# Spectral mixing: batches brought innermost on chip, block-diagonal operand filled by transfers, mirrored columns computed by symmetry

## The chip, the cores and the metric

The kernel runs on one core of one Trainium2 chip, as one program and one launch. The metric is device time in microseconds (us). A core has five engines that each work through their own instructions in order and wait for one another by semaphores: TensorE (PE in the profile; its weight loads are listed as PEld), VectorE (DVE), ScalarE (ACT), GpSimd (POOL) and SyncE (SP), which here only issues transfers. POOL issues transfers too. All transfers of a core run on 16 shared DMA engines. SBUF is the on-chip memory with 128 partitions, called lanes here; PSUM is the memory that TensorE writes its products to.

## The reference

Input `x` has 16 batches, 16 channels and 256 x 256 points. Two residual layers follow each other; the change lies in the first, a pole-residue (Laplace) operator on the group-normalised input:

```python
alpha = jnp.fft.fft2(x, axes=(-2, -1))
A  = 1.0 / (omega1[:, None, None, None] - weights_pole1[None])
Bm = 1.0 / (omega2[:, None, None, None] - weights_pole2[None])
S  = jnp.einsum('ikpq,oikp,xikq->oxik', weights_residue, A, Bm)
output_residue1 = jnp.einsum('biox,oxik->bkox', alpha, S)      # the mix
...
x1 = jnp.fft.ifft2(output_residue1, s=(Ny, Nx), axes=(-2, -1)).real
```

For every frequency (o, x) a 16 x 16 complex matrix `S` mixes the channels i into channels k, for all 16 batches b. As `x` is real, only row frequencies 0 to 128 are computed. The second residual layer (convolutions, mish, an involution and a gate) is not touched.

## The kernel before

`forward` runs four stages one after the other. They hand their data over through tensors in DRAM.

**layer0_forward** (0 to about 1377 us of the profile) computes the spectrum. For every batch b and group of four channels, `rows` transforms the image's rows: products `pu` (L207) with the table `fy`, a copy `right` of one half on ACT (L222), and two additions on DVE (L224) that write the sum and the difference of the two image halves, transposed, into the tile `u`. `columns` (L302 ff.) transforms the other axis from `u` (products `px`, L313), scales on ACT into `o` (L320), and POOL writes `o` to the DRAM tensor `al` (L329). `al` is laid out as group of four row frequencies, real/imaginary part, 64 lanes (row frequency, channel), batch, column frequency.

**layer0_mix** (about 1377 to 2785 us) does the mix in 33 groups g of four row frequencies each. PE, ACT, DVE and POOL follow the order written out by hand at the end of the function (`tc.manual_schedule`). One group consists of:

- `poles(av)`: three DVE products (L640) that spread the pole table into a block-diagonal operand `lt`.
- `residues(lt, s, k0)`, eight times: 16 products of 64 x 32 weights (L656) each, which give the matrices `S` of two output channels; copied to `s` by DVE (L665) or ACT (L667) in turn.
- `spread` and `expand`: the spectrum is loaded from `al` in four quarters of the batches (`alc`, four transfers of 128 KB each, L607, issued by SP), and 16 masked copies (10 on DVE, L619; 6 on ACT, L617) put it into `alb`, the block-diagonal operand: each lane holds one row frequency's channel, and of the four column blocks only its own is not zero. The mask `m4` multiplies the others by zero. `alb` has one buffer.
- `mix(s, y, between)`: 256 products with 128 x 32 weights from `s` and 64 columns from `alb` (L679), in four chunks, each copied to `y` by ACT (L686).
- `turn(y, f)`, four times: eight transposes (L695), copied to `yt` by DVE (L701) and ACT (L699).
- `columns(g, f, yt)`, four times: the inverse transform along the columns. 16 products of 64 x 128 weights with 256 columns of the table `ix` (L714), alternating between lanes 0-63 and 64-127; even and odd points come separately. ACT copies the odd part (L723), DVE writes the sum and the difference (L726, L727) into `o` (tile name `h`, five buffers), and POOL issues four transfers to the DRAM tensor `hd` (L734). For f = 3 the products are interleaved with the next group's `mix` (`between`), behind its second and third chunk.

The stretch from a group's `mix` to the end of its fourth chunk is called the mix section below, and the rest, up to the next `mix`, the f section. In a profile every product of 32-bit numbers appears as two weight loads and two products.

**layer0_back** (2785 to 3422 us) finishes the inverse transform, and **layer1** (3422 us to the end) is the second residual layer.

## Time and profile before

| what | value |
|---|---|
| median of 3 runs | 6919.82 us (6911.33 to 6925.25) |
| the profiled execution's own time | 6939.37 us |
| span of its profile | 6937.6 us |
| mean granted TensorE clock | 0.967 |
| busy in the span: PE, DVE, ACT, POOL | 92%, 79%, 53%, 52% |
| layer0_mix, one group (2003.88 to 2045.67 us) | 41.79 us |
| of it mix section / f section | 16.09 / 25.70 us |
| busy in this group: PE, DVE, ACT, POOL | 36.93, 26.55, 24.32, 13.70 us |

Times of stages are read from tables of busy time by window. A line of a group of instructions gives kernel line, engine, operation, output and inputs, shapes, count, then the time during which at least one of them ran and the mean duration of one, then the idle time of the engine just before them and what ended it. As instructions overlap at their ends, the busy time divided by the count is what one costs in a row, and the mean is what it takes by itself.

### The profile page before, as it was taken

Reading aid. Unit: us, or ns where it says so; the run is one execution under the profiler, and the core shown is the slowest. Engines: PE = TensorE matmul, PEld = TensorE weight load, DVE = VectorE, ACT = ScalarE, POOL = GpSimd, SP = SyncE. Lnnn points to the kernel's source line nnn. Section 1 sums busy time; section 2 is a strip of 40 time slices with the busy share of each in tenths; the row PEclk is TensorE's granted clock in tenths of the full one; section 3 lists DMA queues with packets and bytes.
Section 4 is the critical chain, followed back from the end, with each engine's and each line's share of the span. In section 5 each row is a group of like instructions: output and inputs, shape, how many; then the busy total and the mean of one; then the engine's idle time right before and its main releaser. Section 6 shows DMA issues by size and latency. Waiting matters only on the chain.

```text
span 6937.6 us, 153382 instructions
## 1 busy us (share of the span) xinstructions
PE 6375.2 (92%) x59944; PEld 3583.2 (52%) x59944; DVE 5451.1 (79%) x10057; ACT 3703.9 (53%) x5732; POOL 3635.8 (52%) x4614
## 2 busy tenths in 40 slices
PE   7899989978888888899789999999999999999996
PEld 5777777766766677677533333333333333333331
DVE  8888987356666666788788888888888888888885
ACT  1223333355655555222376666666666666666671
POOL 2334544523333333666665666666766566665563
PEclk9999999989999999999899999999999999999998
DMA  3444434433333333999877898888988889988886
GB/s 95 124 123 122 122 112 119 113 123 104 111 108 111 110 104 93 318 327 326 281 209 231 272 285 261 264 274 277 286 267 261 272 267 285 287 262 262 272 272 211
DMA packets 715941, 1443.97 MB, mean 208 GB/s; under 512 B 101338, under 2 KB 523542, under 8 KB 672950
## 3 DMA queue, kind: packets, MB, share of 16 engines
q1 hardware_dynamic: 567030, 959.77, 45.0%
q0 software_dynamic: 148192, 474.40, 21.8%
q8 instruction: 478, 7.83, 0.5%
q14 instruction: 241, 1.97, 0.1%
HBM read 877.12 MB, written 556.47 MB: 207 GB/s over the span
## 4 chain that ended last, share of the span: by engine, by line
PE 65%; DVE 20%; DMA 5%; issue 5%; ACT 4%; POOL 1%; SPq 0%; DVEq 0%; ACTq 0%; POOLq 0%
PE c2ps L1201 17%; PE c L1053 14%; PE pd L1121 13%; PE pg L679 4%; PE ph L714 3%; DVE alb L619 3%; ACT wide L1101 3%; PE px L313 2%; PE pu L207 2%; PE py L876 2%; PE pr L1080 2%; PE pv L214 2%; DVE u L224 2%; PE py L877 2%; DVE st L174 1%
## 5 line engine op out<-in xcount | busy, mean ns | idle before, releaser
L1101 ACT ACTIVATE wide<-c,b 32x512 f32<-32x512 f32 x2176 | 1479.6, 680 | 311.6 <-PE c L1053 263.5
L1132 DVE TENSOR_TENSOR top<-pd,t 32x512 f32<-32x512 f32 x2176 | 1504.0, 691 | 52.6
L1053 PE MATMUL c<-z,w 102*128 102x512 f32 x2048 | 999.7, 620 | 110.7 <-ACT wide L1101 89.3
L1113 POOL COPY wide<-wide 32x1031 f32<-32x1031 f32 (+1 forms) x576 | 579.7, 1006 | 881.5 <-ACT wide L1101 854.4
L1129 DVE TENSOR_TENSOR t<-pd,r 64x512 f32<-64x512 f32 x1088 | 744.1, 684 | 345.3 <-PE pd L1121 298.2
L1121 PE MATMUL pd<-wide,dw 128*128 128x512 f32 x2048 | 988.6, 604 | 12.0 <-DVE top L1132 11.0
L734 POOL DMA_DIRECT2D hd<-h x512 | 434.8, 856 | 955.0 <-DVE h L727 937.0
L1053 PEld LDWEIGHTS c<-z,w 102*128 102x128 f32 x2048 | 371.7, 192 | 697.5 <-issue 462.5
L1201 PE MATMUL c2ps<-rows,c 128*32 128x512 f32 x6144 | 721.6, 602 | 5.6 <-DVE odd L1228 5.6
L1121 PEld LDWEIGHTS pd<-wide,dw 128*128 128x128 f32 x2048 | 380.9, 192 | 572.2 <-issue 418.5
L1114 POOL COPY wide<-wide 32x1031 f32<-32x1031 f32 (+1 forms) x576 | 576.0, 1000 | 33.5
L1072 ACT ACTIVATE bot<-c,b 128x512 f32<-128x512 f32 x544 | 344.4, 684 | 462.6 <-issue 381.4
L714 PE MATMUL ph<-ix,yt 64*128 64x256 f32 x4128 | 507.9, 394 | 17.6 <-DVE yt L701 14.7
L313 PE MATMUL px<-wxn,u 128*64 128x256 f32 x4224 | 481.5, 379 | 2.4 <-ACT o L320 2.4
L207 PE MATMUL pu<-fy,eo 128*128 128x128 f32 x2048 | 436.2, 297 | 42.0 <-DVE u L224 35.2
L714 PEld LDWEIGHTS ph<-ix,yt 64*128 64x128 f32 x4128 | 419.6, 192 | 89.9 <-ACT s L667 29.6
L679 PE MATMUL pg<-alb,s 128*32 128x64 f32 x16896 | 311.6, 237 | 154.1 <-issue 71.8
L1201 PEld LDWEIGHTS c2ps<-rows,c 128*32 128x32 f32 x6144 | 174.8, 108 | 513.5 <-issue 404.5
L889 POOL TENSOR_TENSOR x<-x,o 128x512 f32<-128x512 f32 x256 | 324.4, 1267 | 217.3 <-DVE o L888 197.5
L619 DVE TENSOR_SCALAR alb<-alc,m 128x1024 f32<-128x1024 f32 x330 | 424.1, 1415 | 0.0
L214 PE MATMUL pv<-at,eo 128*128 128x128 f32 x2048 | 423.0, 291 | 0.0
L726 DVE TENSOR_TENSOR h<-ph,odd 128x256 f32<-128x256 f32 x258 | 113.4, 440 | 389.4 <-ACT odd L723 389.4
(221 smaller groups left out, 11460.2 us busy)
## 6 DMA issues: line engine op xcount, KB each, us to landing
rows<-cf SPq DMA_DIRECT2D x128, 2176.0 KB
z<-zn SPq DMA_DIRECT2D x768, 257.8 KB
cf<-top POOLq DMA_DIRECT2D x512, 240.0 KB, 6.9
cf<-bot POOLq DMA_DIRECT2D x96, 840.0 KB, 10.8
alc<-al SPq DMA_DIRECT2D x528, 128.0 KB
zn<-zb SPq DMA_DIRECT2D x128, 516.0 KB
o<-zn SPq DMA_DIRECT2D x128, 516.0 KB
z<-in_x SPq DMA_DIRECT2D x64, 1024.0 KB
```

The source lines that it names most:

```text
L313: nc.tensor.matmul(ps[64 * k : 64 * k + 64, :, h], lhsT=u[:, h, part, g0 + j + k].rearrange("p f c -> p (f c)"), rhs=wxn[:, h, part], star ...
L619: eng.tensor_scalar(dst, t, m4[:, j : j + 1], None, ALU.mult)
L679: nc.tensor.matmul(ps[32 * q : 32 * q + 32, x], lhsT=s[:, i].rearrange("p v k -> p (v k)"), rhs=alb[:, i].rearrange("p j b -> p (j b)"), s ...
L714: nc.tensor.matmul(ph[q][:, e], lhsT=yt[lanes, i].rearrange("p t k -> p (t k)"), rhs=ix[lanes, i], start=n == 0, stop=n == 3,)
L1053: nc.tensor.matmul(ps[:, a], lhsT=w, rhs=z[:k, c : c + 2, 0:N], start=True, stop=True)
L1101: nc.scalar.activation(self.feat[64 - 32 * q : 96 - 32 * q, f, self.groups[g], :H], ps[q][32 * f : 32 * f + 32], AF.Mish, bias=b1[0][32 * ...
L1113: nc.gpsimd.tensor_copy(flat[0:32, f, 1:m], flat[64:96, f, 0 : m - 1])
L1114: nc.gpsimd.tensor_copy(flat[96:128, f, 0 : m - 1], flat[32:64, f, 1:m])
L1121: nc.tensor.matmul(ps, lhsT=dwt if self.tail else dw, rhs=self.feat[:, f, cs, :H], start=True, stop=True,)
L1129: nc.vector.tensor_tensor(t[64:128], ps[:64], self.r[:, cs], ALU.mult)
L1132: nc.vector.tensor_tensor(self.top[32 * f : 32 * f + 32, cs, q], ps[lanes], t[lanes], ALU.add)
L1201: nc.tensor.matmul(ps[32 * j : 32 * j + 32], lhsT=w[:, blk], rhs=src[:, 4 * j + blk : 4 * j + blk + 4, x : x + H], start=(i, blk) == (0, 0 ...
```

## The change

The mix works on other data layouts, and its hand-written order changes with them.

- **Order of lanes.** In `layer0_forward` the tile `u` keeps the channel ahead of the row frequency, and a lane of the spectrum is now (row frequency, channel) with the frequency slowest in a table order that puts even numbers first. The DVE additions (L224) therefore write runs of four numbers instead of single numbers 64 bytes apart; their reads step through `pu` and `right` by 32 numbers instead of by 128. `al` is laid out anew: runs of 2 KB are written where there were runs of 1 KB, and runs of 1 KB are read where there were runs of 4 KB.
- **Batches innermost, then transfers.** Instead of 16 masked copies, four plain copies (`interleave`: two on DVE, two on ACT) bring the batches innermost into a new tile `alx` (one buffer), from quarters `alc` (two buffers, one transfer of 512 KB each). `place` issues four SBUF-to-SBUF transfers from SP, of 512 KB each, which write only the blocks of `alb` that are not zero: lanes f, f + 4, f + 8, ... go to block f. The zeros are written once, by two memsets ahead of the stage. A group's `place` stands behind the `mix` of the group before.
- **Mirrored columns.** With a transform at half-integer points, the column x and its mirror image differ only by the sign of one part, so `columns` multiplies by 128 columns of `ix` instead of 256. The symmetric and the antisymmetric parts then give all points: DVE writes the sum and (backwards) the difference into a new tile `w`, and one more addition on DVE and one subtraction on POOL make `o` (now four buffers).
- **Order.** `turn(y, f + 1)` is done ahead of `columns(g, f)`; `residues` stand two ahead of each turn, the last one behind the last turn; the copies of `interleave` for group g + 2 stand behind the `columns` of f = 1 and f = 2.

```diff
-                        pu[:, xh, e].rearrange("p v m -> p (v m)"),
+                        pu[:, xh, :, e],
...
-                    u[:, h, :, :64, :, ch],
-                    pu[:, 0].rearrange("p e v m -> p v m e"),
-                    right.rearrange("p e v m -> p v m e"),
+                    u[:, h, :, : NF - 1, ch],
+                    pu[:, 0].rearrange("p v e (m g) -> p v g (e m)", m=2),
+                    right.rearrange("p v e (m g) -> p v g (e m)", m=2),
...
-                    out=al[g0 + k : g0 + n : 2, v, :, b].rearrange("g p x -> p g x"),
-                    in_=o[64 * k : 64 * k + 64, :w, v],
+                    out=al[g0 // 2 + k, :, v, :, b, :w].rearrange("h c g x -> h c (g x)"),
+                    in_=o[64 * k : 64 * k + 64, v, :w].rearrange("p g x -> p (g x)"),
...
-    alb = cp.tile([P, N, 4, nb], F32, name="alb")
+    alb = cp.tile([P, 4, N, nb], F32, name="alb")
+    nc.vector.memset(alb[:, :2], 0.0)
+    nc.gpsimd.memset(alb[:, 2:], 0.0)
...
-        t = gp.tile([P, 4, 2, P], F32, tag="alc", name="alc", bufs=4)
-        src = al[g].rearrange("v (j h c) b x -> h (v j) c (b x)", h=4, c=4)
-        for h in range(4):
+        t = gp.tile([P, 4, N], F32, tag="alc", name="alc", bufs=2)
+        src = al[g // 4 * 2 + g % 2, :, :, :, 4 * q : 4 * q + 4, g % 4 // 2]
+        nc.sync.dma_start(out=t, in_=src.rearrange("h v c b x -> (h v c) b x"))
+        return t
+
+    def interleave(alx, t, q):
+
+        dst, src = alx[:, :, 4 * q : 4 * q + 4], t.rearrange("p b x -> p x b")
+        if q % 2:
+            nc.scalar.copy(dst, src)
+        else:
+            nc.vector.tensor_copy(dst, src)
+
+    def place(alx):
+
+        for f in range(4):
             nc.sync.dma_start(
-                out=t[32 * h : 32 * h + 32].rearrange("p b e x -> p (b e x)"),
-                in_=src[h, :, :, 4 * q * N : 4 * q * N + 4 * N],
+                out=alb[f::4, f].rearrange("p x b -> p (x b)"),
+                in_=alx[f::4].rearrange("p x b -> p (x b)"),
             )
...
-                av[:, :, :, plane].unsqueeze(3).to_broadcast(shape),
-                m16.unsqueeze(1).unsqueeze(2).to_broadcast(shape),
+                av[:, :, :, plane].unsqueeze(2).to_broadcast(shape),
+                m16.unsqueeze(1).unsqueeze(3).to_broadcast(shape),
...
-                        rhs=alb[:, i].rearrange("p j b -> p (j b)"),
+                        rhs=alb[:, :, N // 2 * (i % 2) + i // 2],
...
+            for v in range(2):
+                blocks = slice(0, 4, 3) if v == 0 else slice(1, 3)
+                for c in range(2):
+                    i = 2 * (2 * c + e) + v
+                    for q in range(2):
+                        lanes = slice(64 * q, 64 * q + 64)
+                        nc.tensor.matmul(
+                            ph[q][:, e, blocks],
+                            lhsT=yt[lanes, i].rearrange("p t k -> p (t k)"),
+                            rhs=ix[lanes, i].rearrange("p (b x) -> p b x", b=2),
...
-            odd = hp.tile([P, 2, P], F32, tag="odd", name="odd", bufs=2)
-            nc.scalar.copy(odd, ph[q][:, 1].rearrange("p (v x) -> p v x", v=2))
-            o = hp.tile([P, 2, 2, P], F32, tag="h", name="h", bufs=5)
-            even = ph[q][:, 0].rearrange("p (v x) -> p v x", v=2)
-            nc.vector.tensor_tensor(o[:, :, 0], even, odd, ALU.add)
-            nc.vector.tensor_tensor(o[:, :, 1], even, odd, ALU.subtract)
+            anti = hp.tile([P, 2, 2, 64], F32, tag="anti", name="anti", bufs=2)
+            nc.scalar.copy(anti, ph[q][:, :, 2:])
+            w = hp.tile([P, 2, 2, 2, 64], F32, tag="w", name="w", bufs=2)
+            sym = ph[q][:, :, :2]
+            nc.vector.tensor_tensor(w[:, 0], sym, anti, ALU.add)
+            nc.vector.tensor_tensor(w[:, 1, :, :, ::-1], sym, anti, ALU.subtract)
+            o = hp.tile([P, 2, 4, 64], F32, tag="h", name="h", bufs=4)
+            parts = o.rearrange("p v s x -> p s v x")
+            nc.vector.tensor_tensor(parts[:, 0::3], w[:, :, 0], w[:, :, 1], ALU.add)
+            nc.gpsimd.tensor_tensor(parts[:, 2:0:-1], w[:, :, 0], w[:, :, 1], ALU.subtract)
...
             mix(s, y, between)
             if more:
+                place(alx)
                 s = gp.tile([P, N, 2, C], F32, tag="s", name="s")
                 residues(lt, s, 0)
+                if g + 2 < NF:
+                    av = load_poles(g + 2)
+                    alx = new_alx()
+            last = 3 if more else 0
+            yt = turn(y, 0)
+            for f in range(last + 1):
+                following = None
+                if f < last:
+                    for k0 in (4 * f + 2, 4 * f + 4):
                         residues(lt, s, k0)
+                    following = turn(y, f + 1)
+                    if f == 2:
+                        residues(lt, s, 14)
                 between = columns(g, f, yt)
                 if f < 3:
                     for _ in between:
                         pass
+                if f in (1, 2) and g + 2 < NF:
+                    for q in (2 * f - 2, 2 * f - 1):
+                        interleave_next(alx, q)
+                yt = following
```

`interleave_next` copies the oldest quarter loaded and then issues the load of the next one in the order (group, quarter); two quarters are loaded ahead. The tables `fy`, `wxn`, `ix`, `gc` and the frequency numbers change with the layouts; `m4` goes.

## The prediction

> **What bounds the kernel now.** I read the page's slices first, then busy time by stage, then one group of the mix by windows and groups, last the starts of single weight loads. The stage from 1440 to 2640 us (columns: length, busy PE, PEld, DVE, ACT, POOL, granted clock, DMA share, GB/s), one group's mix section, and its f section:
>
> ```profile
> 1440.00:2640.00 1200.00, 1048.21 (x26413) 841.96 (x26414) 759.74 (x1059) 696.03 (x741) 388.91 (x456) 0.95 0.36 109
> ...
> 2003.88:2019.97 16.09, 13.94 (x544) 12.36 (x544) 3.67 (x8) 3.89 (x6) 0.83 (x3) 0.79 0.28 92
> 2019.97:2045.67 25.70, 22.99 (x385) 17.72 (x385) 22.88 (x30) 20.44 (x21) 12.87 (x15) 1.00 0.43 127
> ```
>
> PE bounds the f section (22.99 of 25.70 us), but DVE (22.88) and ACT (20.44) are nearly as full; in the mix section they stand idle. So a gain must take work from PE and DVE together. The groups of that group g show where it sits:
>
> ```profile
> L714 PE MATMUL ph<-ix,yt 64*128 64x256 f32 x128 | 15.2, 384 | 0.5 <-DVE yt L701 0.5
> L619 DVE TENSOR_SCALAR alb<-alc,m 128x1024 f32<-128x1024 f32 x10 | 12.9, 1418 | 0.0
> L617 ACT ACTIVATE alb<-alc,m 128x1024 f32<-128x1024 f32 x6 | 11.8, 2060 | 0.0
> L679 PE MATMUL pg<-alb,s 128*32 128x64 f32 x513 | 10.4, 251 | 6.1 <-DVE s L665 4.2 <-issue 1.9
> L656 PE MATMUL ps<-tt,lt 64*32 64x256 f32 x256 | 8.1, 380 | 0.3 <-DVE h L727 0.3
> L665 DVE COPY s<-ps 128x1024 f32<-128x1024 f32 x4 | 4.9, 1216 | 1.1 <-PE ps L656 1.1
> L695 PE MATMUL pt<-ident,y 128*128 128x128 f32 x32 | 4.4, 280 | 0.0
> ```
>
> The two lines that the change attacks are the largest of their engines. L679's wait for `s` (some 2.2 us a group) is DVE being late with its masked copies. After that pause the clock drops to half for a while; the same stretch's later parts show it:
>
> ```profile
> 2009.20:2012.00 2.80, 2.79 (x98) 2.62 (x97) 0.00 (x0) 0.00 (x0) 0.00 (x0) 0.52 0.20 73
> 2012.00:2019.97 7.97, 7.70 (x288) 6.51 (x288) 1.42 (x4) 2.88 (x5) 0.66 (x2) 1.00 0.02 4
> ```
>
> **The change, part by part.** All per group, against 41.79 us.
>
> *Columns (PE).* L714 costs 15.2 us / 4 = 3.8 us a call. With 128 columns instead of 256 the products take half, if the weight loads keep up: they still load 128 columns 32 times a call. Two rows decide. Four loads in the two lane halves against two loads in the whole array:
>
> ```profile
> 2030.17 0.33 PEld L714 LDWEIGHTS ph<-ix,yt 64*128 64x128 f32 x4 [0.94 <-ACT s L667]
> ...
> 646.03 0.30 PEld L207 LDWEIGHTS pu<-fy,eo 128*128 128x128 f32 x2 [1.86 <-issue]
> ```
>
> Four took 0.33 us in the halves, two took 0.30 us in the whole array: the halves load side by side, so about 0.055 us each is possible, as much as a halved product needs (3.8 us / 32 / 2 = 0.06). I take 1.9 us a call. The other end is no gain at all (rival A). A rule of the Trainium skill (TensorE: Matmul & The Clock Gate, § LDWEIGHTS (loading the stationary operand)) speaks against the change: a load takes columns / 1.2 ns, however few rows it fills. By it, were loads one after another, a call would keep 32 x 107 ns = 3.4 us and win 0.4 us instead of 1.9; the four loads in 0.33 us contradict only "one after another".
>
> *The masked copies go.* DVE loses 12.9 us, ACT 11.8. In their place two `interleave` copies each. They read single numbers 1 KB apart and write runs of four. No row does just that; between the dense copy of the same size (L665 1.22; L667 1.05 on ACT) and the masked copies (1.42; 2.06), I take the dearer, being strided like them. Upper end for DVE: ACT's 2.06, so +0.65 us per copy.
>
> *New additions.* `w` is two DVE operations as before; the backward one is between L726's 0.43 and the slowest row of that size, L224's 0.59, so 0 to 8 x 0.16 = 1.3 us. The additions that make `o` are new: 8 x 0.42 = 3.4 us on DVE, 8 x 0.73 to 1.27 on POOL (L265's 128x256 and L889's twice as large). POOL's transfers cost 14.3 us now, minimum 0.60 each, so a round of one f on POOL is 2 x 0.73 + 4 x 0.6 to 0.85 = 3.9 to 4.9 us. DVE then has 26.6 - 12.9 + 2.8 + 3.4 = 19.9 us, ACT 24.3 - 11.8 + 4.1 = 16.6, POOL 14.3 + 5.8 = 20. `lt` (L640) gets another operand order, priced 0 to +1 us; it runs in the mix section, where DVE is idle for 12 us.
>
> *f section after.* PE: residues 8.1 + turns 4.4 + three `columns` calls 5.7 = 18.2 us. DVE is nearly in step: its round is s 1.2, yt 0.7, six additions 2.4, and 1.4 more for the copy at f = 1. At f = 2 the last `residues` needs the PSUM buffer that DVE frees behind that copy, which I work out to 1.5 us of PE waiting. 18.2 + 1.5 = 19.7, say 20.0. Before: 25.7.
>
> *Mix section after.* 16.09 - 1.9 (its `columns` call). The 2.2 us wait for `s` lies in the f section's end and is gone there, as `columns(2)` (1.9 us) now covers the copy. L679 takes 10.4 us, against 4 x 1.95 = 7.8 where the clock is full; with the pause gone I count half of that 2.6 as gained. 16.1 - 1.9 - 1.3 = 12.9 us. Ends: 0 and 2.6. Whether PE reads `alb` in runs of 16 columns as fast as 64 in a row, no row shows: I take 0, at worst twice L679's full-clock time (+7.8 us a group, +250 in all, outside my range).
>
> *Place.* Four transfers from SP that wait for `mix`'s last product. What is queued behind them on SP: one `av` load and the `alc` loads, wanted 10 us later or more. Who waits: the next `mix` (20.0 us later), and the copy `interleave` at f = 1 on DVE and ACT, as `alx` has one buffer; behind that copy stand `s`, `yt` and `w`. The trace has no SBUF-to-SBUF transfer. Nearest, the loads of the same 2.1 MB in this stage:
>
> ```profile
> q1 hardware_dynamic: 22832, 66.58, 17.3%
> ...
> hd<-h POOLq DMA_DIRECT2D x512, 128.0 KB, 4.2
> ...
> out_dram<-o POOLq DMA_DIRECT2D x128, 512.0 KB, 8.1
> ```
>
> 17.3% of 1200 us = 208 us for 66.58 MB, so 2.1 MB take 6.6 us; with 4.2 us to land, 11 us. DVE reaches its copy about 15 us after `mix` (residues, two turns, two `columns`, `w`): 4 us of slack. The upper end is 8.1 us each in a row, 32 us (rival B). The loads of `alc` move as many bytes as before; `o` with four buffers is used again two rounds (10 us) later, against 4.9 + 4.2 us for issue and landing.
>
> *Sum of the mix.* 20.0 + 12.9 = 32.9 us, 8.9 less, in 32 whole groups: -285 us.
>
> *Start of the stage.* Masked copies took 1399.5 to 1412.2 us; now two rounds of load and copy (about 8 us) and a `place` of 9 to 11 us: +4 us, ends 0 and +15 (the memsets lie under the loads of tables).
>
> *Forward.* DVE's `u`:
>
> ```profile
> L224 DVE TENSOR_TENSOR u<-pu,right x512: 539/587/615, 68.6 to 1336.2; 128x256 f32<-128x256 f32 x171
> ```
>
> Its writes become runs; reads stay strided. Between L726's 0.43 (dense) and, as a loss, the same distance above 0.59; as writes improve and reads don't, I take 0.54: 512 x 0.045 = 23 us of DVE, half of it on the path (DVE and PE are both about 90% busy there): -12 us, ends -55 and +40. By the Trainium skill (Vector Engine (DVE) Microarchitecture Reference, § 5.2 Measured stream behaviour on trn2), a column costs 1.98 ns with all three streams hopping and 1.76 with the two sources: 256 x 0.22 ns = 0.056 us less each, -14 us in the sum instead of -12. Products `pu`, `pv`, `px` keep their sizes; `al`'s transfers keep their count.
>
> Total: -285 + 4 - 12 = -293 us. Durations are the profiled execution's, which took 6939.37 us, 0.3% above the median of 6919.82; against that median: **6627 us**.
>
> **The rivals.**
> A. Weight loads bind. `columns` stays at 3.8 us a call: +7.6 us a group, 40.5 us. For it: the loads are as many and as wide as before. Against it: four in 0.33 us. 6919.8 - 32 x 1.3 - 8 = 6870 us.
> B. `place` is late, slower than before. If the four transfers go one after another at 8.1 us, `mix` starts 33 us after the last one's end; 33 + 12.9 = 45.9 us a group, +4.1 x 32 + 4 - 12: 7043 us. It decides from the point where `place` takes over 41.8 - 12.9 = 29 us. Against it: 6.6 us by the stage's own loads, which have 32 lanes each as well.
> C. DVE or POOL becomes the bound: backward writes (+1 us in the f section), slow `interleave` (+0.65), POOL's additions at 1.27 us with transfers at 0.85 (a round of 5.9 instead of 5 us, three rounds: +2.7). The masked copies that cover this now are gone. Of these 4.4 us I count three quarters, as they lie partly beside one another: 36.1 us a group, 6730 us.
>
> **How the numbers follow.** Main case 0.62 (its own range 6515 to 6700: a group of 30 us with +4 and -30 beside it, or 34.5 us with +4 and +10), C 0.20, A 0.08, B 0.10. The range takes in the main case and C with C's sum left open upward: 6520 to 6790. About 0.2% can be told from no change here. Main, C and nearly all of A are faster, B slower.
>
> **What would show it.** In the profile after: L708 (`ph`) about half of 15.2 us a group; `alb` copies gone, `alx` copies at 1.2 to 2.1 us; a group of some 33 us; PE's wait for `s` gone; `mix` not waiting for a transfer. I'm wrong if `mix` or `interleave` waits for `alb<-alx`, if `ph`'s loads stand 0.11 us apart, or if L224 gets dearer.

## The result, and the profile after

The changed kernel takes 6946.07 us (median of 13 runs, 6929.2 to 6960.01); the kernel before takes 6918.01 us beside it (median of 13, 6901.41 to 6931.25). The ratio is 1.0041 with a 95% interval of 1.0029 to 1.0052: 0.4% slower, where 6627 us had been forecast. The profiled execution of the changed kernel took 6933.44 us with a span of 6931.7 us.

One sentence of the section on the change has to be corrected: a lane of the spectrum after the change is (channel, row frequency) with the four row frequencies innermost, in the table's order; the frequency is not the slowest.

So a gain and losses of some hundred us nearly cancel. The starts and ends of the products `px` (the forward stage) and `pg` (the mix) place them; sections are means over the 32 whole groups:

| | predicted change | before | after | measured change |
|---|---|---|---|---|
| forward stage, end of the last `px` | -12 | 1377.2 | 1470.1 | +92.9 |
| from there to the first product of the mix | +4 | 35.4 | 39.5 | +4.1 |
| f section, a group | -5.7 | 26.3 | 21.7 | -4.6 (x32: -148) |
| mix section, a group | -3.2 | 15.6 | 17.0 | +1.3 (x32: +42) |

92.9 + 4.1 - 148 + 42 = -9 us; the last group, which the means leave out, and what follows add 3, and the span fell by 5.9 us. `layer0_back` and `layer1` hardly moved: from the last product of the mix to the end of the span it is 4169 us before and 4171 after.

The table of busy time by window of the changed kernel: the stage, then the mix section and the f section of one group (columns: length, busy PE, PEld, DVE, ACT, POOL, granted clock, DMA share, GB/s).

```profile
1520.00:2640.00 1120.00, 896.79 (x26811) 727.41 (x26807) 591.89 (x1066) 485.11 (x636) 545.89 (x686) 0.93 0.55 170
2053.31:2070.77 17.46, 13.48 (x554) 12.43 (x558) 7.56 (x16) 6.39 (x8) 8.27 (x10) 0.79 0.39 121
2070.77:2092.56 21.79, 19.40 (x385) 14.22 (x384) 12.99 (x21) 10.47 (x14) 11.01 (x15) 0.92 0.69 211
```

Against the windows shown of before, DVE's 22.88 us and ACT's 20.44 us in the f section have become 12.99 and 10.47: the masked copies are gone. PE's work fell too. But PE's clock in the f section is no longer 1.00, and the mix section, which lost work, is not shorter. The groups of instructions of the same group g:

```profile
L708 PE MATMUL ph<-ix,yt 64*128 64x128 f32 x130 | 10.9, 312 | 3.1 <-issue 3.1
L671 PE MATMUL pg<-alb,s 128*32 128x64 f32 x512 | 10.2, 246 | 0.9 <-issue 0.9
...
L648 PE MATMUL ps<-tt,lt 64*32 64x256 f32 x256 | 9.0, 412 | 2.3 <-DVE s L657 2.3
...
L614 ACT COPY alx<-alc 128x1024 f32<-128x1024 f32 x2 | 4.2, 2079 | 0.9 <-DMA alc<-al 0.9
...
L616 DVE COPY alx<-alc 128x1024 f32<-128x1024 f32 x2 | 2.5, 1274 | 0.0
```

`columns` (L708) costs 10.9 us a group instead of 15.2, or 2.0 us a call where it runs at full clock. L648 waits 2.3 us for `s`, behind DVE's copy `alx`. And 4 us are lost to "issue", the word for idle time in which the engine waited for no other engine's result. Over all 33 groups the products of the mix (L679 before, L671 after) waited twice as long for issue as before:

```profile
L679 PE MATMUL pg<-alb,s 128*32 128x64 f32 x16896 | 311.6, 237 | 154.1 <-issue 71.8 <-DVE s L665 68.7 <-DMA alc<-al 13.2
L671 PE MATMUL pg<-alb,s 128*32 128x64 f32 x16896 | 312.4, 233 | 155.1 <-issue 148.1 <-ACT y L678 5.0 <-DMA alb<-alx 1.9
```

The timeline of PE in the mix section of that group shows where the gaps lie (start, length, line, count, idle time before):

```profile
2053.31 2.52 PE L671 MATMUL pg<-alb,s 128*32 128x64 f32 x146
2056.29 1.76 PE L671 MATMUL pg<-alb,s 128*32 128x64 f32 x110 [0.46 <-issue]
2057.98 1.16 PE L708 MATMUL ph<-ix,yt 64*128 64x128 f32 x16
2059.07 0.24 PE L671 MATMUL pg<-alb,s 128*32 128x64 f32 x1
2059.74 1.99 PE L671 MATMUL pg<-alb,s 128*32 128x64 f32 x127 [0.43 <-issue]
2061.66 0.37 PE L708 MATMUL ph<-ix,yt 64*128 64x128 f32 x1
2065.13 2.07 PE L708 MATMUL ph<-ix,yt 64*128 64x128 f32 x15 [3.10 <-issue]
2067.13 3.64 PE L671 MATMUL pg<-alb,s 128*32 128x64 f32 x128
```

The gaps are not at the ends of the four chunks (each has 128 products). They stand 110 + 16 + 1 = 127 and 127 + 1 = 128 products apart; with a weight load to each product that is 256 instructions. The table of transfers of the same stretch has a queue that carries instructions:

```profile
q8 instruction: 5, 0.08, 2.0%
```

Five packets in 17.5 us, 16 KB each (0.08 MB). In the whole span that queue moved 478 packets with 7.83 MB, and PE has 59,944 products and as many loads; 7.83 MB / 119,888 is 65 bytes each. So a packet is about 256 PE instructions, the distance of the gaps. This suggested that the mix section is bounded by how fast PE's instructions arrive.

The forward stage had the same order of instructions on every engine, and two lines differed: L224 (`u`) and the transfers L329 (`al<-o`). Their own views after the change, with the shortest, median and longest duration in ns, and with those who waited for `u` (us, times); below each, what the same view has of before:

```profile
L224 DVE TENSOR_TENSOR u<-pu,right x512: 512/590/622, 68.5 to 1423.1; 128x256 f32<-128x256 f32 x171
...
  PE pu L207: 66.3, 36
```

```profile
  PE pu L207: 35.2, 26
```

```profile
DMA to landing us min/median/max: 2.6/4.6/11.0
```

```profile
DMA to landing us min/median/max: 1.9/2.9/8.4
```

By itself an addition `u` takes as long as before (587 and 590 ns), but a busy time of 268.1 us for 512 of them became 286.9: in a row they cost 0.560 us instead of 0.524. PE waits 66.3 us for `u` instead of 35.2. And a write to `al` lands after 4.6 us (median) instead of 2.9, 11.0 at the latest instead of 8.4.

### The profile page after: what moved, and what is told of

It is laid out like the page before. It is cut to its first block, busy times and chain, and to the rows that moved or that the text cites. A ratio compares the mean times of both kernels' runs of the same rounds, so it can differ in the third digit from the quotient of the medians.

```text
span 6931.7 us, 153296 instructions
## 1 busy us (share of the span) xinstructions
PE 6209.0 (90%) x59944; PEld 3454.6 (50%) x59944; DVE 5286.9 (76%) x10052; ACT 3446.3 (50%) x5600; POOL 3830.8 (55%) x4873
## 3 DMA queue, kind: packets, MB, share of 16 engines
q8 instruction: 478, 7.83, 0.5%
## 4 chain that ended last, share of the span: by engine, by line
PE 45%; ACT 3%; DVE 1%; issue 1%; DMA 0%; SPq 0%; POOL 0%; POOLq 0%; DVEq 0%; ACTq 0%
PE c2ps L1216 17%; PE c L1068 14%; PE pd L1136 13%; ACT wide L1116 3%; PE pr L1095 2%; DVE top L1147 0%; DVE pair L1206 0%; DVE t L1144 0%; DMA z<-zn 0%; DVE even L1235 0%; ACT odd L1227 0%; DVE both L1237 0%; ACT bot L1087 0%; DVE odd L1243 0%; DMA o<-zn 0%
## 5 line engine op out<-in xcount | busy, mean ns | idle before, releaser
L725 POOL TENSOR_TENSOR h<-w 128x256 f32<-128x256 f32 x258 | 246.0, 953 | 590.4 <-DVE w L721 588.3
L207 PE MATMUL pu<-fy,eo 128*128 128x128 f32 x2048 | 446.6, 303 | 84.5 <-DVE u L224 66.3
L313 PE MATMUL px<-wxn,u 128*64 128x256 f32 x4224 | 484.3, 380 | 10.9 <-ACT o L320 10.9
L720 DVE TENSOR_TENSOR w<-ph,anti 128x256 f32<-128x256 f32 x258 | 108.4, 420 | 451.9 <-ACT anti L717 451.9
L671 PE MATMUL pg<-alb,s 128*32 128x64 f32 x16896 | 312.4, 233 | 155.1 <-issue 148.1
L732 POOL DMA_DIRECT2D hd<-h x512 | 364.3, 713 | 85.8 <-POOL h L725 38.3
L329 POOL DMA_DIRECT2D al<-o x544 | 340.1, 632 | 128.7 <-ACT o L320 88.4
L320 ACT ACTIVATE o<-px,rsc 128x512 f32<-128x512 f32 (+1 forms) x272 | 185.5, 686 | 434.0 <-PE px L313 351.6
```

Of the source, the lines that this page charges most:

```text
L207: nc.tensor.matmul(pu[:, xh, :, e], lhsT=lhs, rhs=fy[:, e].rearrange("p (v m) -> p v m", v=2), start=True, stop=True,)
L313: nc.tensor.matmul(ps[64 * k : 64 * k + 64, :, h], lhsT=u[:, h, part, g0 + j + k].rearrange("p c f -> p (c f)"), rhs=wxn[:, h, part], star ...
L732: nc.gpsimd.dma_start(out=hd[fy % 2, part, fy % P // 2, q:nb:2].rearrange("b k x -> b (k x)"), in_=o[:, v],)
```

## The experiments

Two questions were open: which of the two edits makes the forward stage longer, and what bounds the mix section. All runs were timed beside the kernel before; ratios are to it, with 95% intervals.

**One edit of the forward stage at a time.**

```diff
-    us = [cp.tile([P, 2, 2, NF, 4, C], F32, name=f"u{i}") for i in range(2)]
+    us = [cp.tile([P, 2, 2, NF, C, 4], F32, name=f"u{i}") for i in range(2)]
...
-                    pu[:, 0].rearrange("p e v m -> p v m e"),
+                    pu[:, 0].rearrange("p v e (m g) -> p v g (e m)", m=2),
```

> The kernel before, with only the layout of the tile u changed as in the kernel after (channel ahead of row frequency, the table fy permuted to match); al, the mix and all else stay. The lanes then hold another order than the mix assumes, so the mix works on wrong lanes; the work is the same. Measured before and after: the forward stage ends at 1377 and about 1470 us, +92 us; the records of L224 stand 0.44 us apart before and 0.51 after. Theory 'reads of u': the strided reads of PSUM and SBUF make DVE's additions dearer, 512 x 0.065 = +33 us of DVE; the stage ends 30 to 45 us later, the kernel takes about 6955 us, and the time from one addition to the next is 0.50 or more. Theory 'transfers to al': the stage ends 0 to 10 us later, the kernel takes 6918 to 6930 us. My prediction on record had -12 us for this edit.

```diff
-    al = dram.tile([NF, 2, 64, nb, N], F32, name="al")
+    al = dram.tile([17, 4, 2, C, nb, 2, N], F32, name="al")
...
-                    out=al[g0 + k : g0 + n : 2, v, :, b].rearrange("g p x -> p g x"),
+                    out=al[g0 // 2 + k, :, v, :, b, :w].rearrange("h c g x -> h c (g x)"),
```

> The kernel before, with only the layout of the DRAM tensor al and of the tile o changed as in the kernel after (runs of 2 KB written with an outermost step of 4, one load of 512 KB a quarter in runs of 1 KB); u and the mix's arithmetic stay. The lanes are loaded in another order than the mix assumes, so the mix works on wrong lanes; the work is the same. Theory 'transfers to al': the transfers' landing rises from a median of 2.9 us to 4.5 or more as it does in the kernel after, the forward stage ends 45 to 60 us later, and the kernel takes about 6970 us. Theory 'reads of u': landing may rise, but the stage ends 0 to 10 us later and the kernel takes 6918 to 6930 us. If the two edits only add up, the stage's delays of this run and of the run with u alone make 92 us together; if each alone is hidden, both are small.

With `u` alone: 6945.99 us, 1.0035 (1.0022 to 1.0048); the forward stage ends at 1397.4 us, +20.2. With `al` alone: 6992.93 us, 1.0102 (1.0084 to 1.0120); it ends at 1444.7 us, +67.5. Together 87.7 of the 92.9 us. Neither theory was right alone: both edits lengthen the stage, their delays add up, and the transfers take three quarters. (The stage's end varies by itself: in four runs that all have the changed kernel's forward stage it lies at 1469.1 to 1480.7 us.) The landing, with `al` alone:

```profile
DMA to landing us min/median/max: 2.6/4.6/11.2
```

With `u` alone it stayed at 3.0 us, and L224's busy time rose to 286.9 us as in the changed kernel; with `al` alone that stayed at 267.6. What waits for a late write is `o`: ACT's wait for `al<-o` rose from 53.2 us to 89.6 with `al` alone, and behind it the whole step.

**What bounds the mix section: half the columns, or half the count.** The first streams 32 of 64 columns of `alb` with as many instructions. The second leaves out every second product and streams 128 columns with the others.

```diff
-                        ps[32 * q : 32 * q + 32, x],
+                        ps[32 * q : 32 * q + 32, x, :32],
...
-                        rhs=alb[:, :, N // 2 * (i % 2) + i // 2],
+                        rhs=alb[:, :2, N // 2 * (i % 2) + i // 2],
```

> The kernel after, with the mix's products streaming 32 of the 64 columns of alb; two of the four row frequencies are left out and their place in y is filled with copies. As many instructions as after. The mix section of a group is 16.7 to 17.4 us after. Theory 'delivery of instructions': 512 weight loads and 512 products a group come no faster than 256 instructions per 3.3 us or so, thus the section keeps its length within 1 us a group and the kernel its 6946 us within 30 us. Theory 'streaming' (reads of alb in runs of 16 numbers are slow, or the products themselves bind): 256 products of two passes lose half of their 10 us or more, the section gets 4 to 5 us shorter, and the kernel takes 6800 to 6820 us.

```diff
-            for x in range(16):
+            for x in range(0, 16, 2):
...
-                        ps[32 * q : 32 * q + 32, x],
+                        ps[32 * q : 32 * q + 32, x : x + 2].rearrange("p x (f b) -> p f x b", f=4),
...
-                        rhs=alb[:, :, N // 2 * (i % 2) + i // 2],
+                        rhs=alb[:, :, k : k + 2],
```

(In the second, `k` is `N // 2 * (i % 2) + i // 2`.)

> The kernel after, with every second product of the mix left out and the others streaming 128 columns of alb (two neighbouring column frequencies with the weights of the first) instead of 64: half as many instructions and the same number of streamed columns; the results of every second column frequency use wrong weights. It is the counterpart of the run with half the columns and the same count, whose mix section stayed at 17.0 us. Theory 'delivery of instructions': 512 instructions fewer a group at 3.3 us per 256 make the section 6 to 7 us shorter, 10 to 11 us, and the kernel takes 6730 to 6760 us. Theory 'streaming': the section keeps 16 to 17 us and the kernel its 6946 us within 30 us. Another possibility is that the mix section then waits for ACT's copies y: about 12 to 13 us.

Half the columns: the mix section is 17.0 us (mean of 32 groups), as with all of them; the kernel takes 6969.29 us, 1.0069 (1.0048 to 1.0090). Half the count: the mix section is 10.3 us, 6.7 less, and the kernel takes 6740.20 us, 0.9735 (0.9720 to 0.9749). One mix section of each by window, first with half the columns, then with half the count:

```profile
2028.67:2045.72 17.05, 10.06 (x554) 9.23 (x560) 5.97 (x13) 6.20 (x8) 5.88 (x7) 0.70 0.51 179
```

```profile
1999.58:2009.23 9.65, 9.65 (x298) 8.81 (x303) 6.60 (x14) 6.27 (x8) 6.50 (x7) 1.00 0.59 180
```

With half the columns PE is busy for 10 of 17 us. Its timeline in that section has the same distances, 67 + 16 + 44 = 127 products between two gaps:

```profile
2028.67 1.82 PE L671 MATMUL pg<-alb,s 128*32 128x32 f32 x189
2033.39 0.78 PE L671 MATMUL pg<-alb,s 128*32 128x32 f32 x67 [2.90 <-issue]
2034.11 1.93 PE L711 MATMUL ph<-ix,yt 64*128 64x128 f32 x16
2035.97 0.85 PE L671 MATMUL pg<-alb,s 128*32 128x32 f32 x44
2040.91 1.39 PE L671 MATMUL pg<-alb,s 128*32 128x32 f32 x84 [4.09 <-issue]
```

With half the count PE has no gap in this section, and the full clock. So the mix section waits for instructions: in the windows shown 1112 and 1114 of them take 17.46 and 17.05 us, 4.0 and 3.9 us for each 256, whether they stream 64 columns or 32. That a packet is 256 PE instructions shows here too: the run with half the count has 16,896 of them fewer in its trace, and 66 packets fewer on the queue (412 instead of 478).

The time for each 256 is no constant. As many instructions took 15.6 us before the change, 3.7 us for each 256. In the mix sections of the changed kernel the instruction packets start 3.6 us apart (median) where other transfers fill less than 30% of the 16 DMA engines meanwhile (packets under way; 48 intervals), and 5.1 us where they fill over half (45); with half the columns it is 3.5 and 5.9, but before the change 3.75 and 3.65. A packet itself takes about 1 us in both kernels. Transfers beside them may thus delay the packets, and part of the 1.3 us may come from there; no run varied that alone.

The doubt whether PE reads `alb` in runs of 16 numbers as fast as before is settled too: in the timeline of the changed kernel 127 products take 1.99 us, where the prediction had 1.95 us for 128 at full clock.

The Trainium skill ("Advanced Engine Details and Errata", § ISA Cache) has a cache line of 16 KB for 256 instructions; the distance of the gaps and the size of the packets agree with it.

**DVE's copies in front of `s`.**

```diff
-        if q % 2:
-            nc.scalar.copy(dst, src)
-        else:
-            nc.vector.tensor_copy(dst, src)
+        nc.scalar.copy(dst, src)
```

> The kernel after, with all four copies of interleave on ACT instead of two on DVE. PE waits some 2.3 us a group for s behind DVE's copy at f = 2, and the clock is at half for a while after it. Theory 'DVE's copy stands in front of s': the wait shrinks below 1 us, the f section from 21.9 to about 20 us or less, and the kernel takes 6850 to 6880 us. Theory 'other' (ACT's copies of 2.06 us stand in front of the odd s and of yt instead, or the wait comes from the order of residues): PE waits as long as before, in other places, and the kernel stays within 6930 to 6990 us.

6860.85 us, 0.9907 (0.9891 to 0.9922). The f section falls from 21.7 to 20.2 us, the mix section from 17.0 to 15.9, a group from 38.65 to 36.03. PE's waits ahead of `residues` in the whole kernel, first in the changed kernel, then with this edit; and the f section of one group:

```profile
L648 PE MATMUL ps<-tt,lt 64*32 64x256 f32 x8448 | 283.5, 390 | 108.5 <-DVE s L657 87.0 <-DVE lt L632 10.5 <-issue 9.6
L645 PE MATMUL ps<-tt,lt 64*32 64x256 f32 x8448 | 281.5, 386 | 76.3 <-DVE s L654 38.9 <-ACT s L656 14.1 <-issue 12.7
```

```profile
2086.12:2105.22 19.10, 17.85 (x386) 13.40 (x385) 12.13 (x21) 12.38 (x15) 11.44 (x17) 1.00 0.74 214
```

The clock is 1.00 again; from the first product of the mix to the last it stood at half for 5.8% of the time, against 13.6% in the changed kernel. So one DVE copy in front of `s` cost its wait and then a stretch at a lower clock (in the changed kernel 0.63 from 2088.03 to 2092.56 us, behind a wait of 2.32 us for `s`). The shorter mix section comes with it, though its own instructions are the same; that the clock alone does this was not tried by itself.

**Reading `pu` without gaps.**

```diff
-            pu = psu.tile([P, 2, 2, 2, 64], F32, tag="pu", name="pu")
+            pu = psu.tile([P, 2, 2, 32, 4], F32, tag="pu", name="pu")
...
-                        pu[:, xh, :, e],
+                        pu[:, xh, :, :, 2 * e : 2 * e + 2],
...
-    fy = fy.reshape(P, 2, 2, 32, 2).swapaxes(3, 4)
```

> The kernel after, with the columns of the table fy reordered so that TensorE writes pu in the order in which u wants it (row frequency group, then the four frequencies): L224 and the copy right read dense numbers, and only u's writes keep gaps. In the run with u alone L224's records stood farther apart and the forward stage ended 20 us later. Theory 'strided reads': with dense reads L224's busy time falls from 287 us to 240 or less, and the forward stage ends 20 us or more earlier than after's 1470 us, so the kernel takes 6915 to 6930 us. Theory 'short writes' (runs of four numbers with gaps are what is dear): L224 stays at 0.5 us or more apart and the kernel at 6940 to 6950 us. TensorE writing pairs with gaps could also cost: L207 would then rise from 447 us.

6890.33 us, 0.9958 (0.9943 to 0.9973). The forward stage ends at 1420.5 us, 50 earlier than in the changed kernel:

```profile
L224 DVE TENSOR_TENSOR u<-pu,right x512: 363/417/427, 68.1 to 1373.4; 128x256 f32<-128x256 f32 x171
```

417 ns where both layouts before had 587 and 590, and a busy time of 197.6 us instead of 286.9. Writing `pu` in pairs with gaps costs PE nothing (L207: 436.7 us, against 446.6). The change had turned the writes of `u` into runs of four numbers, as intended, but the reads still took single numbers with steps of 128 bytes; with steps left on that side, L224 gained nothing.

**The layout of `al` as before.** This puts `al` and `o` back and loads a quarter in four transfers. The next two runs combine it with the two edits above, the second of them with more products between the chunks of the mix.

```diff
-        src = al[g // 4 * 2 + g % 2, :, :, :, 4 * q : 4 * q + 4, g % 4 // 2]
-        nc.sync.dma_start(out=t, in_=src.rearrange("h v c b x -> (h v c) b x"))
+        src = al[g, :, :, 4 * q : 4 * q + 4].rearrange("v (h c) b x -> h v c (b x)", h=4)
+        for h in range(4):
+            nc.sync.dma_start(out=t[32 * h : 32 * h + 32].rearrange("p b x -> p (b x)"), in_=src[h])
```

> The kernel after, with the DRAM tensor al and the tile o laid out as before the change (64 lanes as the outer step of a write, runs of 1 KB); each quarter is then loaded by four transfers of 128 KB in runs of 4 KB. In the run with al alone the forward stage ended 67 us later than before. Theory 'transfers to al': their landing falls from 4.6 back to 2.9 us, the forward stage ends at 1400 to 1410 us, and the kernel takes 6875 to 6890 us. Rival: the loads of alc, now four a quarter, come later and cost the mix some of it: a group above 38.65 us.

> The kernel after with three edits together: all copies of interleave on ACT, pu in u's order, al as before. If they add up: 6946 - 85 - 65 - 20 = about 6775 us, with the forward stage ending at 1375 to 1395 us and a group of 36.0 us. If ACT, which issues the copies that free what the forward stage and the mix wait for, takes something back, up to 6810 us.

> The combined kernel, with the products of columns for f = 2 also placed between the chunks of the next mix, in four pieces, one ahead of each chunk. Theory 'delivery of instructions': the mix section waits for instructions, and the products of columns, long for each instruction, run while these arrive; so the section keeps 15.8 us though it holds 1.9 us more work, the f section loses 1.5 to 2 us, a group takes 34 to 34.5 us, and the kernel some 6715 to 6725 us. Theory 'mix section is full of work': it grows by 1.9 us and the group keeps 36 us. Rival: without columns in front of it, the mix waits for the last copy s, up to 1.2 us a group, which takes back half or more.

7426.25 us, 1.0734 (1.0718 to 1.0750); combined 7401.80 us, 1.0697 (1.0681 to 1.0713); with more between 7425.38 us, 1.0733 (1.0716 to 1.0751). The write side did what was expected: landing is 3.0 us and the forward stage ends at 1401.0 us, 69 earlier (1343.9 with `pu` in order). But a group of the mix takes some 55 us. ACT's copies of `alx`, over 1000 us of the mix in the first of these runs:

```profile
L615 ACT COPY alx<-alc 128x1024 f32<-128x1024 f32 x36 | 72.2, 2005 | 425.1 <-DMA alc<-al 311.5 <-DMA alb<-alx 100.7 <-issue 12.9
```

The bytes and packets of a load are those of the kernel before (32 packets of 4 KB a transfer). What differs is the shape on the DRAM side: here a transfer steps outermost by the two parts `v`, before by 8 (two parts times four row frequencies). I added up the durations of the packets of these loads and divided by the time from the first to the last: 1.9 packets were under way at a time, against 4.8 to 5.7 before the change, and about 10 in the changed kernel, whose load steps by 128 lanes. The writes to `al` differ in the same way: in the changed kernel they step outermost by 4, before by 64. Their packets show it too: each write of 128 KB comes with 96 packets of 8 bytes in the changed kernel, three for each of its 32 packets of 4 KB, and with none before. Four engines with data and twelve without would make that ratio; the trace does not name the engines. A rule of the Trainium skill fits the loads and the writes ("DMA: Bandwidth & Descriptors", § Rules for kernel authors): an outermost dimension of size c below 16 confines a transfer to c engines at most. 1.9 for a size of 2 agrees with it. The rival of the first expectation, slower loads, decided the result. With the loads that slow, the run with more products between the chunks says nothing about the mix section.

**Sixteen in front.** `u` holds the channels as (within the group of four, row frequency, group), so that the lanes of a write go to DRAM with 16 as the outermost step; `al` and its loads stay as in the changed kernel. All copies are on ACT and `pu` is in order here too.

```diff
-                    u[:, h, :, : NF - 1, ch],
+                    u[:, h, :, : NF - 1, ch % 4, :, ch // 4],
...
-                    out=al[g0 // 2 + k, :, v, :, b, :w].rearrange("h c g x -> h c (g x)"),
+                    out=al[g0 // 2 + k, :, v, :, b, :w].rearrange("h c g x -> c h (g x)"),
```

> The kernel after with three edits together: all copies of interleave on ACT; pu written in u's order; and the lanes of the spectrum ordered so that a write to al has 16 as its outer step on the DRAM side instead of 4 (u is stored as channel within its group of four, row frequency, group of four), while al keeps its layout and its one load of 512 KB a quarter. Theory 'outer step': the runs so far had transfers whose DRAM side steps outermost by 2, 4, 8 and 128, and they kept 1.9, about 4, 5 and 10 DMA engines busy; with 16 the landing of al<-o falls from 4.6 to about 3 us and the stage's end moves 65 to 70 us earlier, to 1355 to 1385 us counting pu's order, with a group of 36.0 us: 6950 - 85 - 50 - 65 = about 6750 us. Rival: landing stays at 4.6 us, as the run length or the order of al itself makes it dear; the kernel takes about 6810 us. L224 now writes single numbers 16 bytes apart; if it is dearer than the 0.39 us a piece of the run with dense reads, up to +20 us.

6761.91 us, 0.9766 (0.9751 to 0.9781): faster than both kernels, by 2.3% than before. The forward stage ends at 1364.7 us, and a group takes 36.4 us. L224, and the landing of the writes to `al`:

```profile
L224 DVE TENSOR_TENSOR u<-pu,right x512: 551/600/632, 68.3 to 1324.5; 128x256 f32<-128x256 f32 x171
```

```profile
DMA to landing us min/median/max: 1.8/2.5/7.1
```

Landing is better than before the change, in runs of the same length as in the changed kernel, and the packets of 8 bytes are gone. So the outermost step, and not the length of the runs, made the writes late. L224 is back at 600 ns, with dense reads: now its writes are single numbers, 16 bytes apart. Its busy time is 272.9 us, 75 more than with writes in runs of four; the stage ends 21 us later than in the combined kernel, which has such writes, about the 20 that I had allowed.

**More products between the chunks.** The kernel just shown, with the products of `columns` for f = 2 put between the chunks of the next mix too.

```diff
-            if x0 >= 32:
-                next(between, None)
+            next(between, None)
...
+        yield
...
-                if f < 3:
+                if f == 2:
+                    held = between
+                elif f == 3:
+                    between = chain(held, between)
+                else:
                     for _ in between:
                         pass
```

> The kernel with the outer step of 16 and its two other edits, with the products of columns for f = 2 also placed between the chunks of the next mix, in four pieces, one ahead of each chunk. Theory 'delivery of instructions': products of columns run long for each instruction, while those of the mix arrive; the section keeps 15.8 us though it holds 1.9 us more work, the f section loses 1.5 to 2 us, a group takes 34 to 34.5 us and the kernel 50 to 60 us less than without. Theory 'mix section is full of work': the group keeps 36 us. Rival: the mix now waits for the last copy s, up to 1.2 us a group, which takes back half or more.

6769.56 us, 0.9786 (0.9770 to 0.9802): no gain. The mix section grew from 16.1 to 17.3 us, where it had been expected to keep its length, and the f section fell from 20.3 to 19.4 only. The line of `columns` over 1000 us of the mix, first without, then with the edit:

```profile
L705 PE MATMUL ph<-ix,yt 64*128 64x128 f32 x3504 | 248.9, 290 | 16.4 <-issue 15.7 <-ACT yt L688 0.7
```

```profile
L705 PE MATMUL ph<-ix,yt 64*128 64x128 f32 x3504 | 264.9, 291 | 48.6 <-DVE w L718 40.4 <-issue 7.3 <-ACT yt L688 0.7
```

The products of the mix (L668) wait 68.8 us for issue instead of 110.3, as expected. But `ph` now waits 40.4 us for `w` on DVE, which frees one of its two buffers: the products stand closer behind the `columns` before them. These waits are as long as the gain at the mix's products; a wait of the mix for the copy `s`, which I had named, does not appear. More buffers for `ph` were not tried.

**Sixteen in front for the loads.** The combined kernel of 7401.80 us, with each quarter loaded in eight transfers of 16 lanes.

```diff
-        for h in range(4):
-            nc.sync.dma_start(out=t[32 * h : 32 * h + 32].rearrange("p b x -> p (b x)"), in_=src[h])
+        for k in range(8):
+            h, v = k // 2, k % 2
+            nc.sync.dma_start(
+                out=t[16 * k : 16 * k + 16].rearrange("p b x -> p (b x)"),
+                in_=al[g, v, 16 * h : 16 * h + 16, 4 * q : 4 * q + 4].rearrange("p b x -> p (b x)"),
+            )
```

> The combined kernel that took 7402 us (al as before, pu in u's order, all copies of interleave on ACT), with each load of a quarter cut into eight transfers of 64 KB instead of four of 128 KB, so that a transfer's DRAM side steps outermost by 16 lanes instead of by 2 parts. Same bytes, same runs of 4 KB, twice as many transfers. Theory 'outer step': two engines a transfer were the whole cause of the 55 us a group; with 16 the loads of a quarter land in about 7 us, the wait of the copies alx for alc (some 645 us in all) falls below 60 us, a group takes 36 to 37 us, and with a forward stage that ends at 1344 us the kernel takes 6725 to 6755 us. Rival 'too many or too long transfers': if runs of 4 KB or the issues on SP (0.59 us each, 19 us a group for 32 of them) are what is slow, the group stays above 42 us and the kernel above 6930 us.

6778.01 us, 0.9803 (0.9786 to 0.9819). The same bytes in the same runs, in twice as many transfers, and 624 us are back: the shape was the main cause. But a group takes 37.5 us, and ACT still waits for the loads:

```profile
L617 ACT COPY alx<-alc 128x1024 f32<-128x1024 f32 x104 | 207.9, 2028 | 129.2 <-DMA alc<-al 129.1
```

5.7 packets are under way at a time, not 10, and the expectation of 6725 to 6755 us was missed. SP takes 0.42 us to issue a transfer (median); 16 packets of some 0.2 us every 0.42 us make about 8 at most. So the number of transfers may limit here too; what holds it at 5.7 was not tried.

## Why the prediction was wrong, point by point

- **"`al`'s transfers keep their count"** was costed at nothing, and is the largest error of the forward stage: +67.5 us with that edit alone. The transfers kept their count and bytes and got longer runs, but their outermost step went from 64 to 4, and the landing from 2.9 to 4.6 us. The prediction looked at the lanes of `place` and of the loads beside it, and at the shape of no transfer that touches the new `al`. With 16 in front the landing is 2.5 us.
- **Forward, `u`: -12 us.** Sign and size were wrong: +20.2 us with that edit alone, inside the stated ends of -55 and +40. The step that failed is "as writes improve and reads don't, I take 0.54": with reads still in steps nothing improves: by itself an addition took 0.59 us as before, and in a row 0.56 instead of 0.52. The Trainium skill's rule that was weighed there ("Vector Engine (DVE) Microarchitecture Reference", § 5.2 Measured stream behaviour on trn2) gave an estimate of -14 us by 1.98 against 1.76 ns a column; this case measured no such gain, and the measurement decides.
- **Mix section: 12.9 us.** It measured 17.0, the largest part of the error. Both terms failed: "-1.9 (its `columns` call)" and "with the pause gone I count half of that 2.6 as gained". The section was not filled by its work. It waits for instructions, so the work taken out of it came back as waiting; with half the streaming it still took 17.0 us, with half the instructions 10.3. The signs were on the page: L679 had 1.9 us of "issue" in its wait, which I did not follow up. That the section even got 1.3 us longer is only partly explained: the run with all copies on ACT has 15.9.
- **f section: 20.0 us.** It measured 21.7. The mechanism (`residues` behind DVE's copy at f = 2) was right, its size wrong: 2.3 us for "1.5", and then a clock of 0.92 instead of the full clock that the sum took for granted. Without DVE's copies the section measured 20.2.
- **Columns: 1.9 us a call.** 2.0 measured where the clock is full. Its 32 loads thus stand 0.06 us apart, side by side as the prediction read them; an estimate by the rule of "TensorE: Matmul & The Clock Gate", § LDWEIGHTS (loading the stationary operand), with one load after another, is 3.4 us. Rival A is out.
- **Copies and `place`.** `alx` cost 1.24 us on DVE and 2.10 on ACT (1.42 and 2.06 were taken). `mix` waited 1.9 us for `alb<-alx` in the whole kernel, so `place` is hidden, and rival B is out. The backward `w` costs no more than the forward one (0.41 and 0.42 us), POOL's subtraction 0.95, within 0.73 to 1.27. The 14.3 us for POOL's transfers count one transfer of the group beside; the window has 13.70.
- **Rival C** (DVE becomes the bound) had the right place, a copy in front of what PE waits for, and with the half clock it is worth 85 us, the gain of the run with all copies on ACT. Its time of 6730 us left out the forward stage and the mix section.
- **Start of the stage: +4 us.** 4.1 measured. The parts of this sum were not measured singly, so the agreement may be luck.

The sum is off by 105 us in the forward stage, 145 in the mix section and 34 in the f section, together 284; the spans are off by 287 (-293 forecast, -5.9 measured).

## What to carry to other kernels

Before shortening the work of a stretch, see whether that work fills it: many small products can wait for their own instructions, which shows as "issue" gaps at equal counts (256 instructions here), and then less streaming does not shorten it. Half the instructions did here; longer ones put between them met a new wait. When a layout changes, look at every transfer that touches it, and at its outermost step on the DRAM side rather than at its bytes or runs. The addition here that hopped on one side was not made faster by runs on the other side alone; it was when the engine before it wrote the order in which it is read.

## What the runs showed of the hardware

- PE's instructions arrive in packets of 16 KB, 256 instructions; in the mix section of the changed kernel 256 took 3.9 to 4.0 us, whether each product streamed 32 or 64 columns.
- Loads of the same bytes and run length kept 1.9 packets under way with an outermost step of 2 and 5.7 with 16 in transfers half as large; the kernel took 7402 and 6778 us.
- A write of 128 KB to DRAM with an outermost step of 4 landed after 4.6 us (median) and came with 96 packets of 8 bytes; with a step of 64 or 16 it landed after 2.9 and 2.5 us and had none.
- A two-source addition of 256 columns on DVE, one source in PSUM, took 587 to 600 ns with hops between single numbers on one side or both, and 417 ns with dense reads and writes in runs of four.
- A wait on PE can cost more than itself: with DVE's copies on ACT, PE's waits for `s` fell from 87.0 us (on DVE) to 53.0 (38.9 on DVE, 14.1 on ACT), by 34 us, and the kernel by 85; the share of half clock fell from 13.6% to 5.8% of the mix.
